# Exact 16-bit row reordering, wide sums over slots and a new step order in a four-layer graph kernel

## The chip, the cores and the metric

The kernel runs on one core of a Trainium2 chip. The metric is the device time of one execution in microseconds, the median over runs. PE is the matrix engine (TensorE; PEld is its loading of weights), DVE the vector engine, ACT the scalar engine, POOL the GpSimd engine, and SP the engine that here only issues transfers.

## The reference

Sixteen graphs (batches) of N = 1024 nodes with C = 64 channels go through four graph layers. Each layer is added to its input and followed by a layer norm over the 64 channels. The adjacency `adj` is 16 x 1024 x 1024, not symmetric in its values, symmetric in its pattern, with the diagonal set and below one per cent of the other entries filled.

```python
x = layernorm(x + (adj @ (x @ W0) + b0))                       # layer 0
# layer 1: Chebyshev, K = 4
z0, z1 = x, adj @ x;  z2 = 2*adj @ z1 - z0;  z3 = 2*adj @ z2 - z1
x = layernorm(x + sum(z_k @ theta[k]))
# layer 2: for each node the multiset of its neighbours' rows (diagonal included);
# where there are over 10 neighbours, every skip-th edge is dropped, in both directions
agg = 0.25*quantile(rows, 0.25) + 0.5*quantile(rows, 0.5) + 0.25*quantile(rows, 0.75)
x = layernorm(x + mask * (relu((x + agg) @ W1 + b1) @ W2 + b2))
# layer 3: batch norm over all 16 * 1024 rows, then (I - D^.5 adj D^-.5)
x = layernorm(x + leaky_relu((I - An) @ (batchnorm(x) @ W3 + b)))
```

The quantiles are taken in each channel by itself, with linear interpolation between sorted values, so layer 2 has to fetch the rows of each node's neighbours and sort them.

## The kernel before

Nodes are tiled as 8 chunks (`NK`) of 128 partitions. One batch passes through nine generators, each of which issues its instructions in steps that end in a `yield`:

- `rows in` loads the adjacency by rows of chunks, turns it on PE (L476) and evacuates it on ACT (L477) into `f_adj_t`, kept in fp32. For each chunk ACT also makes a key of the row's signs (L497), DVE multiplies it by a band of node numbers (L499) and takes the largest eight of each 128 columns (L502), which gives each node's list of neighbours.
- `layers` computes layers 0 and 1. A product with the adjacency is a "hop" (L451): 16 fp32 matmuls of 512 moving columns, `f_adj_t` moving and the node values as weights. Its last step norms the rows into `xr` and writes them to DRAM as `rows`.
- `lists` turns each node's neighbours into a record of row numbers, sorts the nodes by their number of neighbours, and computes each node's `place`. Steps `at0` to `at7` make a one-hot matrix on DVE for each chunk (L701, f16, 128 x 1152), with which PE moves the records (L705) and the node rows `xr` (L725) into the sorted order. For L725 ACT first casts the one-hot to fp32 (L722). Step `ids` (13) copies the row numbers out (L736 is the copy of `meta`); step `own` (14) turns the reordered rows into `xs`.
- `fetch` issues the gathers on POOL (L768): indirect transfers of 128 rows each from `rows`, 70 in a batch (3 + 12 in steps 0 to 2, 37 in steps 3 to 10, 18 in steps 11 to 14).
- `heads` prepares the gathered rows: dead slots, interpolation weights, and the copies on ACT (L839) from the gather buffers `got` into `home`. A next batch's gather into the same buffer waits for these.
- `sorts` sorts the slots on DVE, 128 partitions at a time (L869), in three classes of chunks (1, 4 and 3 chunks, with 24, 11 and 8 slots), multiplies by the weights (L883), and sums over the slots on PE (L893) into the PSUM bank `xt`. There the slots' values are the weights of the array (64 or 128 columns, one or two chunks), and a scaled identity of 128 columns moves: the sum comes out already turned, with channels on partitions.
- `ends` copies `xt` (L908), runs the perceptron of layer 2 (L913 and on) and norms into `x3p`.
- `back` undoes the sorting: a row of places, eight one-hots on DVE (L961, f16), a cast on ACT (L963), and two fp32 matmuls (L966) for each. The last step copies the result, channels on partitions, into `f_x3t` (L971).
- `third` loads the turned adjacency again from DRAM (step 0), scales the rows into the weights `u` (step 1, L994 and on, with the statistics L988), does the hop of layer 3 (step 2, copied by ACT at L999), scales (step 3) and writes out (step 4).

All instructions are issued in one written order. Step u of generator g in batch b has the due time `b * PERIOD + WHEN[g][u]`, and the steps of all batches are issued sorted by it:

```python
for name, part in (...):
    parts += [(b * PERIOD + when, b, name, u, part) for u, when in enumerate(WHEN[name])]
for _, b, name, u, part in sorted(parts, key=lambda p: p[0]):
    next(part)
```

The due times only set the order of each engine's queue; nothing waits for a clock. `PERIOD` is 120 in units of the plan. A step that is written earlier on an engine holds all that follow on it until its inputs are there. Around the release of the gathers of batch b the order is: `lists[b]` 13, `back[b-2]` 7 to 10, `lists[b+1]` 1 and 2, `sorts[b-1]` 83 to 110 with `lists[b]` 14, `third[b-2]` 1, `layers[b+1]` 1 and 2, `lists[b+1]` 3, `heads[b-1]` 7 among them, then `third[b-2]` 2 (the hop) and `rows in[b+2]` 1.

Each PSUM bank name stands for one bank, except for two banks each of `l0` and `turn`; `end` serves `ends`, `back` and `third`. The buffers `at16` and `at32` have two copies each.

After the last batch the batch norm and the final norm of all batches follow ("fin", L1619 to L1712), with POOL doing two 128 x 512 operations a batch (L1689, L1705). A slow path for graphs with too many neighbours is built in and not taken with these inputs.

Of the kernel before, what the change touches and what calls it, by code (L numbers as in the profile page):

```python
# [10 lines left out]
F32 = mybir.dt.float32  # L11
# [8 lines left out]
P = 128  # L20
# [155 lines left out]
def _strides(slots):  # L176

    out, rest = [], list(slots)
    while rest:
# [13 lines left out]
PERIOD = 120  # L193

WHEN = {
    "rows in": (-248.4, -220, -217.5, -211.2, -206.1, -201.4, -197.3, -189.6, -181.9, -172.4),
    "layers": (-135.2, -116.7, -104.1, -98.7, -95, -86.9, -83, -79.2, -69.6, -67.9, -63, -56.1),
    "lists": (-134.5, -130.9, -129, -114.6, -64.7, -48, -48, -39.8, -39.8, -34.9, -31.5, -24.3, -19.3, -14.4, -4.6),
    "fetch": (6.9, 14.8, 29.3, 29.3, 29.3, 33.6, 39.4, 42.9, 72, 72, 88.8, 96.5, 105.4, 108, 110.5),
    "heads": (41.2, 50.2, 51.6, 89.4, 102.9, 106.2, 109.8, 132.9, 144.8, 154.8),  # L200
    "sorts": (
        58.3, 58.3, 58.3, 59.6, 59.6, 63.2, 64.7, 64.7, 64.7, 64.7, 64.7, 64.7, 64.7, 64.7, 64.7, 64.7, 72.1, 74.9,
        75.8, 76.2, 76.2, 76.2, 76.2, 76.2, 76.6, 76.6, 76.6, 76.6, 78.4, 78.7, 78.7, 79.6, 79.9, 80.5, 80.8, 80.8,
        80.8, 84.4, 85, 85, 85.9, 86.4, 86.4, 87.6, 87.6, 87.6, 88.5, 89.1, 89.1, 89.1, 89.1, 89.8, 89.9, 89.9,
        90.9, 90.9, 90.9, 91.6, 91.6, 91.6, 91.6, 91.6, 92.6, 92.7, 95.1, 95.1, 95.1, 95.2, 95.2, 98.6, 98.6, 98.6,
        99.6, 100.6, 101.1, 102.8, 103, 103, 103, 103, 103, 103, 103, 112.3, 113, 113.3, 113.3, 120.9, 122.3, 127,
        127, 129.6, 129.6, 133.4, 134.1, 134.1, 134.1, 135.8, 137.3, 137.3, 137.3, 137.3, 137.3, 137.3, 137.3,
        137.3, 137.3, 137.3, 137.3, 137.3, 137.3, 141.1, 141.1, 141.1, 141.1, 141.1, 146.8, 157.7, 157.7, 158, 158,
        158, 158, 158, 159.1, 162.4, 163.6, 163.6, 163.6, 165.1, 168.3, 168.3, 169.2, 172.4,
    ),  # L210
    "ends": (181.3, 188.1, 197.1, 207.7),
    "back": (149.8, 155.7, 209.3, 209.7, 211.2, 212.4, 212.9, 228, 229.8, 231.4, 231.4),
    "third": (222.8, 241.8, 258.3, 262.5, 291.8),
# [4 lines left out]
def gnn_layers_kernel(  # L218
# [261 lines left out]

# [43 lines left out]
    def layers(b, st, pw):  # L524
# [60 lines left out]
        nc.scalar.dma_start(out=rows[N : N + 1], in_=big_row)  # L585
        st.update(rows=rows)
        yield "rows"

    def lists(b, st, pw):

        mask = mask_t[:, b * NK : (b + 1) * NK]
# [1151 lines left out]
```

## Time and profile before

| what | value |
|---|---|
| median of 14 runs | 2976.2 us (2961.8 to 2981.37) |
| profiled execution, its own time | 2961.18 us |
| its span in the profile | 2959.4 us |
| mean granted clock of PE | 0.772 |
| busy: PE, DVE, ACT, POOL | 1880.9, 1889.4, 1457.0, 1195.3 us |
| gathers (L768 into `got`) | 1072, 1034 ns each |
| casts to fp32 (L722, L963) | 128 + 128, 1042 ns each |

The profile is of one execution. Busy times are summed over all instructions of an engine, without the instructions that only wait, branch or issue transfers. A row of the groups of instructions gives line, engine, operation, what is written from what, shape and count, then the busy time in us and the mean of one in ns, then the engine's idle time just before these instructions with what ended it. "Issue" as a releaser is time in which the engine waited for nothing that the profile shows, "remote" an event that could not be put to an instruction. An fp32 matmul of this kernel is recorded as two records, so the 512 records of L725 are 256 matmuls. The windows by stage give, for a stretch of the span, the busy time and the number of instructions of each engine, the granted clock, the share of busy DMA engines and their GB/s.

### The profile page before, as it was taken

The page shows a single profiled execution, that of the slowest core. Times are in us where ns is not written, and L with a number is a line of the kernel's source. Part 1 is how long each engine was busy: PE and PEld are TensorE (multiplying, and loading weights), DVE is VectorE, ACT ScalarE, POOL GpSimd, SP SyncE. Part 2 cuts the span into 40 slices and gives each one's busy share as a digit, 9 for nine tenths or more (in the row PEclk, how much of TensorE's full clock was granted, in tenths as well). Part 3 has the DMA queues.
Part 4 walks back from the last instruction along what each step waited for, and adds up shares of the span by engine and source line. Part 5 has one row for each costly group of instructions (what it writes and reads, how often), then busy time and mean ns, then how long its engine had stood idle before and what let it go on. Part 6 is the DMA issues. An engine that isn't in the chain of part 4 may idle for free. (4 is left out here: it accounts for less than half of the span.)

```text
span 2959.4 us, 33419 instructions
## 1 busy us (share of the span) xinstructions
PE 1880.9 (64%) x9766; PEld 950.6 (32%) x9766; DVE 1889.4 (64%) x5870; ACT 1457.0 (49%) x4405; POOL 1195.3 (40%) x1159
## 2 busy tenths in 40 slices
PE   5727366776758485775848576675848677663553
PEld 3303242423324152332414242342415243232233
DVE  6507576684939487584938567593948668372826
ACT  4505355563736365463726456373726556362533
POOL 0260725436162725426162633616162543626004
PEclk9957687887969697786958788786969788776675
DMA  4322232242424133242414124242414223121126
GB/s 160 119 40 104 43 126 68 60 151 53 154 46 164 31 117 95 60 150 49 156 43 165 35 73 137 59 148 47 162 31 144 69 61 133 21 77 30 58 81 160
DMA packets 130464, 272.28 MB, mean 92 GB/s; under 512 B 77024, under 2 KB 77280, under 8 KB 120032
## 3 DMA queue, kind: packets, MB, share of 16 engines
q1 hardware_dynamic: 57536, 218.90, 19.9%
q0 software_dynamic: 35840, 37.92, 8.2%
q10 hardware_dynamic: 36896, 13.23, 1.8%
q8 instruction: 79, 1.29, 0.2%
q14 instruction: 113, 0.93, 0.1%
HBM read 185.89 MB, written 84.07 MB: 91 GB/s over the span
## 5 line engine op out<-in xcount | busy, mean ns | idle before, releaser
L768 POOL DMA_INDIRECT got<-rows,ids x1072 | 1108.5, 1034 | 559.0 <-issue 252.2
L451 PE MATMUL ps_end<-f_adj_t,f_u 128*64 128x512 f32 x512 | 263.1, 853 | 332.8 <-issue 297.6
L768 POOL DMA_INDIRECT extra<-rows,more x48 | 49.0, 1021 | 1019.4 <-ACT meta L736 1009.7
L499 DVE TENSOR_TENSOR key<-key,keyband 128x1024 f16<-128x1024 f16 x128 | 88.4, 690 | 534.2 <-ACT key L497 524.7
L451 PE MATMUL ps_l<-f_adj_t,f_t 128*64 128x512 f32 x1536 | 371.6, 631 | 34.5 <-issue 34.5
L839 ACT ACTIVATE home<-got,big 128x64 f32<-128x64 f32 x1344 | 332.5, 338 | 0.0
L476 PE MATMUL ps_turn<-cf,f_a 128*128 128x128 f32 x1024 | 190.8, 323 | 185.9 <-issue 158.9
L869 DVE TENSOR_TENSOR away<-home 128x768 f32<-128x768 f32 (+9 forms) x416 | 230.6, 574 | 46.1 <-ACT home L839 21.8
L476 PEld LDWEIGHTS ps_turn<-cf,f_a 128*128 128x128 f32 x1024 | 138.0, 163 | 271.8 <-issue 230.8
L451 PEld LDWEIGHTS ps_end<-f_adj_t,f_u 128*64 128x64 f32 x512 | 59.0, 181 | 510.9 <-issue 472.0
L477 ACT COPY f_adj_t<-ps_turn 128x512 f32<-128x512 f32 x256 | 139.3, 595 | 169.1 <-PE ps_turn L476 74.9
L502 DVE MAX8 cand<-key 128x8 f16<-128x128 f16 x1024 | 210.8, 280 | 5.3 <-issue 0.9
L966 PE MATMUL ps_end<-at,f_h 128*64 128x512 f32 x512 | 149.3, 684 | 91.2 <-issue 48.9
L999 ACT COPY f_ht<-ps_end 128x512 f32<-128x512 f32 x16 | 9.4, 586 | 393.8 <-remote 238.3
L725 PE MATMUL ps_px<-at,xr 128*64 128x512 f32 x512 | 176.7, 776 | 31.8 <-ACT at L722 31.3
L451 PEld LDWEIGHTS ps_l<-f_adj_t,f_t 128*64 128x64 f32 x1536 | 113.4, 145 | 258.8 <-issue 256.5
L893 PE MATMUL ps_xt<-quarter,home 128*128 128x128 f32 (+1 forms) x1088 | 165.5, 290 | 17.8 <-DVE home L883 17.8
L869 DVE TENSOR_TENSOR home<-away,home 128x128 f32<-128x128 f32 (+5 forms) x352 | 165.5, 474 | 9.5 <-remote 2.7
L893 PEld LDWEIGHTS ps_xt<-quarter,home 128*128 128x128 f32 (+1 forms) x1088 | 140.7, 185 | 44.2 <-DVE home L883 41.6
L722 ACT CAST at<-at 128x1024 f32<-128x1024 f16 x128 | 130.4, 1042 | 49.5 <-DVE at L701 31.9
L497 ACT ACTIVATE key<-f_a 128x1024 f16<-128x1024 f32 x128 | 136.2, 1064 | 33.5 <-DVE cand L502 18.1
L869 DVE TENSOR_TENSOR home<-away 128x64 f32<-128x64 f32 (+7 forms) x304 | 149.2, 509 | 1.1
(236 smaller groups left out, 3335.6 us busy)
## 6 DMA issues: line engine op xcount, KB each, us to landing
f_a<-in_adj_dram SPq DMA_DIRECT2D x128, 512.0 KB
adj<-f_adj_t SPq DMA_DIRECT2D x16, 4096.0 KB
f_adj_t<-adj SPq DMA_DIRECT2D x64, 1024.0 KB
got<-rows,ids POOLq DMA_INDIRECT x1072
rows<-xr ACTq DMA_DIRECT2D x16, 264.0 KB
f_x<-in_x_dram ACTq DMA_DIRECT2D x16, 256.0 KB
x_d<-f_x SPq DMA_DIRECT2D x16, 256.0 KB
z_d<-f_ht SPq DMA_DIRECT2D x16, 256.0 KB
```

Source lines behind the costliest of these rows:

```text
L451: nc.tensor.matmul(ps[h * C : (h + 1) * C, :], lhsT=v[:, j, :], rhs=pairs[:, j, h], start=(j == 0), stop=(j == NK - 1),)
L476: nc.tensor.transpose(pt[:, j * P : (j + 1) * P], a[:, (4 * g + j) * P : (4 * g + j + 1) * P], ident)
L477: nc.scalar.copy(adj_t[:, 4 * g : 4 * g + 4, i * P : (i + 1) * P], pt.rearrange("p (j n) -> p j n", n=P))
L497: nc.scalar.activation(flat_key, a, AF.Sign)
L502: nc.vector.max(out=cand[:, i, j * 8 : j * 8 + 8], in_=key[:, j, :])
L722: nc.scalar.copy(at_32, at_place[:, 0:N])
L725: nc.tensor.matmul(po[h * C : (h + 1) * C, :], lhsT=xr[:, k, 0:C], rhs=pairs[:, h], start=(k == 0), stop=(k == NK - 1))
L768: nc.gpsimd.indirect_dma_start(out=w[0], out_offset=None, in_=rows[:, :], in_offset=bass.IndirectOffsetOnAxis(ap=w[1], axis=0))
L839: nc.scalar.activation(home[:, s + 1, k, :], got[:, s, k, 0:C], AF.Identity, bias=big_dead[:, s, k : k + 1], scale=1.0,)
L869: nc.vector.tensor_tensor(out=at(ho, r1 if is_max else r0, *run), in0=at(ha, r0, *run), in1=at(hb, r1, *run), op=ALU.max if is_max else AL ...
L893: nc.tensor.matmul(st["xt"][h * C : (h + n) * C, q * P : (q + 1) * P], lhsT=flat(xs[:, k : k + n, :] if s == nr else home[homes[s]][:, s, ...
L966: nc.tensor.matmul(ps[h * C : (h + 1) * C, :], lhsT=x3p[:, k, :], rhs=pairs[:, h], start=(k == 0), stop=(k == NK - 1))
```

## The change

Three things are changed.

First, the reordering in `lists` and `back` no longer casts the one-hot to fp32. The rows are split instead into three bf16 terms whose sum is the fp32 value exactly: the upper 16 bits of each number, read in place; the upper 16 bits of the rest (`mid`); and what is left (`low`). POOL computes the two differences (`in_three`), in a new last step of `layers` for `xr` and in the last step of `ends` for `x3p`. `reordered` then issues for each chunk six matmuls with a bf16 term as weights and the f16 one-hot moving.

Second, the sums over slots in `sorts` keep the scaled identity as weights and move all chunks of a class at once (64, 256 or 192 columns). The sum now comes out with nodes on partitions, so `ends` gets a new first step `summed`, which copies the bank and turns it on PE before the perceptron; the order of chunks in the perceptron's matmuls follows.

Third, `PERIOD` becomes 110 and all due times are new; `layers` and `ends` have one step more. Around the release of the gathers of batch b the order is then: `lists[b]` 13 and 14, `back[b-2]` 10, `layers[b+1]` 1, `lists[b+1]` 2, `sorts[b-1]` 84 to 112 with `third[b-2]` 1, `fetch[b]`'s first steps, `back[b-1]` 0, `lists[b+1]` 3 and `layers[b+1]` 2 among them, then `third[b-2]` 2 and `rows in[b+2]` 1. The two POOL steps lie at 57.5 (`layers` 12) and 63.7 (`ends` 4) of the period of 110, with `fetch` 10 and 11 between them.

```diff
-PERIOD = 120
+PERIOD = 110
 
 WHEN = {
-    "rows in": (-248.4, -220, -217.5, -211.2, -206.1, -201.4, -197.3, -189.6, -181.9, -172.4),
-    "layers": (-135.2, -116.7, -104.1, -98.7, -95, -86.9, -83, -79.2, -69.6, -67.9, -63, -56.1),
-    "lists": (-134.5, -130.9, -129, -114.6, -64.7, -48, -48, -39.8, -39.8, -34.9, -31.5, -24.3, -19.3, -14.4, -4.6),
-    "fetch": (6.9, 14.8, 29.3, 29.3, 29.3, 33.6, 39.4, 42.9, 72, 72, 88.8, 96.5, 105.4, 108, 110.5),
-    "heads": (41.2, 50.2, 51.6, 89.4, 102.9, 106.2, 109.8, 132.9, 144.8, 154.8),
+    "rows in": (-220.5, -212.9, -206.9, -203.9, -199.1, -190.5, -182, -178.6, -172.8, -161),
+    "layers": (-122.6, -117.9, -111.4, -102.8, -96.5, -91.4, -84.2, -73.4, -69.9, -66, -64.6, -60.7, -52.5),
+    "lists": (-127.9, -124, -117.5, -113, -95.9, -50.7, -49.5, -43.5, -39.9, -39.9, -39.5, -35, -19.2, -10.1, -10.1),
+    "fetch": (-4.2, -2.9, -2.9, 7.2, 9, 34.9, 51.2, 51.2, 51.2, 54.6, 62.1, 63.1, 68.7, 68.7, 94.1),
+    "heads": (18.9, 37.8, 38.3, 70.2, 76, 76.2, 84.2, 117.4, 134, 135.7),
     "sorts": (
...
     ),
-    "ends": (181.3, 188.1, 197.1, 207.7),
-    "back": (149.8, 155.7, 209.3, 209.7, 211.2, 212.4, 212.9, 228, 229.8, 231.4, 231.4),
-    "third": (222.8, 241.8, 258.3, 262.5, 291.8),
+    "ends": (155.2, 157.2, 158.6, 168, 173.7),
+    "back": (106.3, 175.1, 185.4, 193.9, 197.8, 199.3, 201.3, 201.7, 208.5, 208.5, 210.4),
+    "third": (207, 215.2, 224.8, 232.6, 245.1),
 }
@@ -478,6 +478,30 @@
 
     flat = lambda t: t.rearrange("p k c -> p (k c)")
 
+    def upper(t, n=C):
+        return t.bitcast(BF16)[:, :, 1 : 2 * n : 2]
+
+    def in_three(pw, x, tag):
+
+        mid = pw.tile([P, NK, C], F32, name=f"{tag}_mid")
+        nc.gpsimd.tensor_tensor(out=mid, in0=x[:, :, 0:C], in1=upper(x), op=ALU.subtract)
+        low = pw.tile([P, NK, C], BF16, name=f"{tag}_low")
+        nc.gpsimd.tensor_tensor(out=low, in0=mid, in1=upper(mid), op=ALU.subtract)
+        return upper(x), upper(mid), low
+
+    def reordered(ps, parts, hot, k):
+
+        pairs = hot.rearrange("p (q h n) -> p h q n", h=2, n=P)
+        for i, part in enumerate(parts):
+            for h in range(2):
+                nc.tensor.matmul(
+                    ps[h * C : (h + 1) * C, :],
+                    lhsT=part[:, k, :],
+                    rhs=pairs[:, h],
+                    start=(k == 0 and i == 0),
+                    stop=(k == NK - 1 and i == 2),
+                )
+
     def rows_in(b, st, keyband, pa, pw):
 
         x0 = pw.tile([P, NK, C], F32, name="f_x0")
@@ -585,6 +609,8 @@
         nc.scalar.dma_start(out=rows[N : N + 1], in_=big_row)
         st.update(rows=rows)
         yield "rows"
+        st.update(x_parts=in_three(pw, xr, "x"))
+        yield "parts"
 
     def lists(b, st, pw):
 
@@ -718,13 +744,7 @@
                 stop=(k == NK - 1),
             )
 
-            at_32 = pw.tile([P, N], F32, name="at32", bufs=2)
-            nc.scalar.copy(at_32, at_place[:, 0:N])
-            pairs = at_32.rearrange("p (q h n) -> p h q n", h=2, n=P)
-            for h in range(2):
-                nc.tensor.matmul(
-                    po[h * C : (h + 1) * C, :], lhsT=xr[:, k, 0:C], rhs=pairs[:, h], start=(k == 0), stop=(k == NK - 1)
-                )
+            reordered(po, st["x_parts"], at_place[:, 0:N], k)
             yield f"at{k}"
         ids = pw.tile([P, NK, OTHERS], I32, name="ids", bufs=AHEAD + 2)
         nc.scalar.copy(ids, pr[:, :, 0:OTHERS])
@@ -884,28 +904,25 @@
 
             if "xt" not in st:
                 st["xt"] = bank("xt")
-            k = k0
-            while k < k0 + nk:
-                n = 2 if k % 2 and k + 1 < NK else 1
-                q, h = ((k - 1) // 2, 0) if n == 2 else (NK // 2 - 1, 1 if k else 0)
-                cols = slice(k - k0, k - k0 + n)
-                for s in range(nr + 1):
-                    nc.tensor.matmul(
-                        st["xt"][h * C : (h + n) * C, q * P : (q + 1) * P],
-                        lhsT=flat(xs[:, k : k + n, :] if s == nr else home[homes[s]][:, s, cols, :]),
-                        rhs=ident if s == nr else quarter,
-                        start=(s == 0),
-                        stop=(s == nr),
-                    )
-                k += n
+            for i in range(nr + 1):
+                nc.tensor.matmul(
+                    st["xt"][:, k0 * C : (k0 + nk) * C],
+                    lhsT=ident if i == nr else quarter,
+                    rhs=flat(xs[:, kk, :] if i == nr else home[homes[i]][:, i]),
+                    start=(i == 0),
+                    stop=(i == nr),
+                )
             yield f"sums{k0}"
 
     def ends(b, st, pw):
 
         meta, xs = st["meta"], st["xs"]
         xt = st.pop("xt")
+        xn = pw.tile([P, 512], F32, name="f_ht", bufs=2)
+        nc.scalar.copy(xn, xt)
+        yield "summed"
         xt_s = pw.tile([P, 512], F32, name="f_h")
-        nc.scalar.copy(xt_s, xt)
+        nc.scalar.copy(xt_s, turned(xn, "xt"))
         ht = []
         for h in range(2):
             hp = slice(h * C, (h + 1) * C)
@@ -923,7 +940,7 @@
             stop=False,
         )
         for k in range(NK):
-            h, q = {0: (0, 3), 7: (1, 3)}.get(k, (1 - k % 2, (k - 1) // 2))
+            h, q = k % 2, k // 2
             nc.tensor.matmul(
                 ph[:, k * C : (k + 1) * C], lhsT=ht[h][:, q * P : (q + 1) * P], rhs=w2_c[:, 0, :], start=False, stop=(k == NK - 1)
             )
@@ -934,7 +951,7 @@
         nc.vector.tensor_tensor(out=h, in0=h, in1=xs, op=ALU.add)
         x3p = h
         yield from norm(pw, x3p, [h], "n2", centred=True)
-        st.update(x3p=x3p)
+        st.update(x3p=in_three(pw, x3p, "x3"))
         yield "x3p"
 
     def back(b, st, pw):
@@ -959,13 +976,7 @@
         for k in range(NK):
             at_node = pw.tile([P, N + P], F16, name="at16", bufs=2)[:, 0:N]
             nc.vector.tensor_scalar(out=at_node, in0=row, scalar1=node[:, k : k + 1], scalar2=None, op0=ALU.is_equal)
-            at_32 = pw.tile([P, N], F32, name="at32", bufs=2)
-            nc.scalar.copy(at_32, at_node)
-            pairs = at_32.rearrange("p (q h n) -> p h q n", h=2, n=P)
-            for h in range(2):
-                nc.tensor.matmul(
-                    ps[h * C : (h + 1) * C, :], lhsT=x3p[:, k, :], rhs=pairs[:, h], start=(k == 0), stop=(k == NK - 1)
-                )
+            reordered(ps, x3p, at_node, k)
             yield f"order{k}"
         xt = pw.tile([P, 512], F32, name="f_x3t")
         nc.scalar.copy(xt, ps)
```

## The prediction

> **What bounds the kernel now.** I read the busy times first, then the waits, then the windows by stage, and last the groups of instructions with their forms.
>
> The busy times of the whole span name no bound: no engine is above 64%.
>
> ```profile
> PE 1880.9 (64%) x9766; PEld 950.6 (32%) x9766; DVE 1889.4 (64%) x5870; ACT 1457.0 (49%) x4405; POOL 1195.3 (40%) x1159
> ```
>
> So the kernel must have stages with different bounds. The step `ids` (L736) of a batch releases the gathers of that batch (L768); call its time T. In the trace it ends at 128.3 for the first batch and at 2636.5 for the last: a period of (2636.5 - 128.3) / 15 = 167.2 us. The windows cut one period (T = 1471 to the next T = 1639) and the end of the one before it.
>
> ```profile
> engine line waited for: us in total, times, longest us
> POOL extra L768 <- ACT meta L736: 1009.7, 16, 122.9
> DVE key L499 <- ACT key L497: 524.7, 35, 56.5
> PEld ps_end L451 <- issue: 472.0, 310, 5.9
> ...
> PE ps_end L451 <- issue: 297.6, 159, 5.5
> POOL got L768 <- ACT home L839: 248.6, 54, 15.0
> ACT f_ht L999 <- remote: 238.3, 9, 48.5
> ```
>
> ```profile
> 1376.00:1471.00 95.00, 81.54 (x501) 43.28 (x501) 85.23 (x287) 68.73 (x201) 20.89 (x18) 0.92 0.41 146
> 1471.00:1495.00 24.00, 12.44 (x68) 7.36 (x66) 19.59 (x54) 14.32 (x46) 18.62 (x18) 0.70 0.24 47
> 1495.00:1545.00 50.00, 21.33 (x41) 5.66 (x42) 9.38 (x19) 6.22 (x27) 33.29 (x35) 0.57 0.15 24
> 1545.00:1639.00 94.00, 79.57 (x474) 41.09 (x474) 80.77 (x267) 63.76 (x179) 21.15 (x18) 0.89 0.41 147
> ```
>
> The columns are PE, PEld, DVE, ACT and POOL busy, the granted clock, the DMA share and GB/s. Three parts are seen. From T to T+24 all engines work. From T+24 to T+74 POOL runs gather after gather while PE ends 41 matmuls in 50 us and ACT 27 instructions; PE waits for nothing that the profile shows ("issue"), in the hop of `third` at L451. In the trace single records of that hop lie 2.8 us apart, and the copy behind it (ACT L999) is released at T+73.7 in every steady batch. Behind L999 in ACT's queue stands the key activation L497, and DVE stands at L499: 524.7 us over 16 batches. From T+74 to the next T (94 us) the work is dense: DVE is busy for 81 to 85 of 94, PE for 80, ACT for 64 to 69. DVE bounds this part, at 0.88 of its time.
>
> What ends the stall? The unbroken stream of gathers has 52 in a steady batch, 61 in the second and 70 in the first; L999 is released at T+73.7, T+86.6 and T+98.6: about 1.41 us for each gather, plus 0.4. The streams of 9 gathers later in the period, with breaks between, slow the others by 2 to 4 us only. I infer that a long stream of gathers slows the issue of the other engines; the trace shows the coincidence and not the mechanism.
>
> So period = stall end + (DVE's work of a batch - what DVE did before the stall end) / 0.88. In the period shown DVE did 19.59 + 9.38 = 29.0 before the stall end: 74 + 80.77 / 0.86 = 168.
>
> **Part by part.**
>
> ```profile
> L768 POOL DMA_INDIRECT got<-rows,ids x1072 | 1108.5, 1034 | 559.0 <-issue 252.2 <-ACT home L839 248.6 <-DMA got<-rows,ids 46.0
> L725 PE MATMUL ps_px<-at,xr 128*64 128x512 f32 x512 | 176.7, 776 | 31.8 <-ACT at L722 31.3
> L963 ACT CAST at<-at 128x1024 f32<-128x1024 f16 x128 | 130.5, 1042 | 21.1 <-DVE at L961 8.5 <-issue 4.9 <-PE ps_end L966 3.7
> L722 ACT CAST at<-at 128x1024 f32<-128x1024 f16 x128 | 130.4, 1042 | 49.5 <-DVE at L701 31.9 <-PE ps_px L725 17.2
> L893 PE MATMUL ps_xt<-quarter,home 128*128 128x128 f32 x704 | 102.2, 294 | 1.9 <-DVE home L883 1.8
> L908 ACT COPY f_h<-ps_xt 128x512 f32<-128x512 f32 x16 | 9.6, 600 | 17.6 <-remote 9.4 <-PE ps_xt L893 8.2
> L1689 POOL TENSOR_TENSOR hf<-hf,s 128x512 f32<-128x512 f32 x16 | 16.7, 1042 | 178.2 <-ACT s L1685 178.2
> ```
>
> The casts go: 16 in a batch at 1042 ns, 16.7 us of ACT. They lie in the dense part, where ACT has 25 to 30 us idle, so their direct worth is nothing; DVE's own waits for them are small (10.3 us in all at L961, 4.5 at L701, 0.9 a batch). If DVE were not the cover, they would be worth the full 16.7.
>
> The reordering matmuls: four f32 records for each k become six of one pass each. In bursts the trace places 32 f32 records of 512 columns in 7.1 us, 0.22 each, and the four of L725 take 1.1 us. For one-pass matmuls of 512 columns no burst is shown; the ends are 0.11 (half of the f32 pace) and 0.22, so six take 0.65 to 1.3. I take 0.65: two passes make one f32 product. PE gains 0.45 x 16 = 7 us a batch, or loses 3.5. It has 14 us free in the dense part, so either end costs at most 1 us.
>
> The sums: 112 records a batch become 76, wider by up to 4 times in columns. The old bursts place 40 records of 128 columns in about 5 us; the new ones move in total nearly the same columns. I take -2 us of PE, hidden as well (ends -5 and +3).
>
> `ends`: a copy like L908 (0.60) and four transposes (a batch of four f32 transposes is about 0.9 us apart from start to end, single records up to 0.42), with their hand-overs, lengthen the chain by 2.5 us. DVE has the sorts of the next batch queued beside it; I take 0, and 2.5 if that cover is gone.
>
> `in_three`: four POOL instructions of 128x512 a batch at 1042 ns (L1689), 4.2 us, perhaps 6 with the strided 16-bit operand. POOL is idle for 70 of the 94 us of the dense part. At0's matmuls (`lists` 5) wait on two of them, and order0's on the other two; what is queued behind those matmuls on PE is delayed by 2 to 3 us once each if POOL is just then in a gather. I take 1 us a batch, ends 0 and 6.
>
> Against these instructions speaks a rule of the Trainium skill ("SBUF — State Buffer", section on the two separate sides): VectorE and GpSimd share one pair of ports as an exclusive lock, taken for a whole instruction when a VectorE operation has two SBUF inputs and the GpSimd operation reads SBUF. The trace shows something like it on POOL's side only: gathers start 1.25 us apart while DVE idles and up to 1.8 while it works, and DVE's own 128x768 steps take 953 or 967 ns without and with gathers. By the rule, DVE would be held for all of POOL's 4.2 us in a batch, 63 us over 15 periods.
>
> The new order matters most, since it decides what stands in front of the stall. DVE's queue between `ids` and the first L499 block held, before: three one-hots of L961 (1.4), `lists` 1 and 2 (5.5), `sorts` 83 to 110 (19.9), the norm's and the heads' small steps (3.0): 29 to 30. After: only `lists` 2 (3.0), `sorts` 84 to 112 (19.2), the small steps (2.5 to 3): 25. The stream after `ids` is 50 gathers instead of 52 (`lists` 13 and the fetch steps stand so that two steps of gathers come later), so the stall ends at 1.41 x 50 + 0.4 = T+71, 2.8 us sooner. And PE has less in front of the hop: `back` 7 to 9 with its matmuls and casts is done before `ids`. The hop can start at about T+14 instead of T+21 to T+25, and takes 7 to 10 us at full pace. The slow part began at T+24 in steady batches. If the hop is through by then, L999 no longer holds ACT's queue; `rows in` 1, `heads` 7 and `sorts` 113 to 114 run too, some 7 us of DVE, and 32 are done by T+71.
>
> The sum, likeliest case: stall end -2.8, dense part -(32 - 29) / 0.88 = -3.4, POOL +1: -5.2 a period, 15 periods -78. At the ends of the run I count +5: the last batch's unbroken stream is 5 gathers longer (+6.7) and `ends` +2.5, `back` -4. The profiled execution took 2961.2 (span 2959.4): 2961 - 73 = 2888. The median of the runs shown is 2976.2, 1.005 of it, so 2888 x 1.005 = 2903; I say 2905. With 1 us either way in each of the three terms it reaches from 2865 to 2945.
>
> **The rivals.**
>
> *The hop is still caught (slower).* Its weights u come from ACT steps after `third` 1, which in the trace lag by 1 to 5 us at T+12 to T+20. If it has not ended when the slow part begins, L999 holds ACT until T+71, and only 25.5 us of DVE work lie in the stall: -2.8 + 3.5 / 0.88 + 1 = +2.2 a period, +33, +5 at the ends: 2999, times 1.005 = 3014; with 1 us either way 2990 to 3035. It decides from a hop end later than T+24. For it speaks that batch 0's slow part began at T+8 to T+18, with DVE idle; against it that steady batches have DVE busy then.
>
> *POOL's instructions hold others.* Streams of 7 and 13 gathers, with `in_three` between and without the pauses for L839, could slow the dense part as the last unbroken 18 gathers did in this trace (a gap of 10 us on DVE). At 5 to 10 us a period: 3050 to 3130. Against it speak the short gaps beside 9 gathers.
>
> *The dense part shrinks with the plan.* If ACT's and PE's relief lets DVE run at 0.95 of the dense part instead of 0.88, that part loses a further 6 us a period: 2800 to 2830. Against it: DVE's waits there are 4 us of small pauses and few waits for ACT.
>
> *It does nothing:* terms cancel, 2970 to 2982.
>
> **How the numbers follow.** The likeliest case, 0.45; the plan's case, 0.10; the hop caught, 0.30; POOL in the way, 0.10; nothing, 0.05. Faster by over 0.2%: the first two, and a sliver of the third, 0.56. Within 0.2% (6 us, about what a measurement of this kernel can tell from no change): 0.06. Slower: 0.38. The range leaves out the plan's case for the most part and POOL's: 2830 to 3035.
>
> **What would show it.** Right: the period between two `ids` is 161 to 163; L999 is released before T+25; L497 is no longer held until the gathers end; the first L499 runs inside the stream; DVE's busy time between T and T+71 is 31 to 33. The 256 casts are gone and ACT's busy time falls by about 250 us without the span following. The reordering takes 0.65 us for each k. Wrong: L999 still lies at T+71 with 25 us of DVE before it (the first rival), DVE gaps beside POOL's TENSOR_TENSOR or DVE steps that last 1 us longer (the second), or a stall end that does not follow the number of gathers: then the term of 1.41 us each fails and all cases move.

## The result and the profile after

The changed kernel takes 3237.6 us, the median of 10 runs (3228.8 to 3267.8), against 2972.8 for the kernel before over 47 runs: 1.090 times the time before, with a 95% interval of 1.088 to 1.093. It was forecast at 2905, between 2830 and 3035. The profiled execution took 3274.1 (span 3272.3). Here and below, runs that took over 1.5 per cent longer than the fastest run of the same kernel are left out of times and ratios.

The busy times of the profile after:

```profile
PE 1847.8 (56%) x9766; PEld 1015.2 (31%) x9766; DVE 1946.9 (59%) x5870; ACT 1207.2 (37%) x4165; POOL 1249.5 (38%) x1223
```

ACT has lost its 256 casts and 250 us, DVE has gained 58 us, and the span has grown by 313. In this section and below, T is the end of ACT's copy of `meta` (L756 after, L736 before), which releases a batch's gathers. The period between two T is 194.5 in the steady part (167.2 before). The windows of one period from T = 1421 (the last 7 us left out), columns as in the prediction:

```profile
1421.00:1445.00 24.00, 11.55 (x83) 8.37 (x83) 16.31 (x50) 4.10 (x17) 18.48 (x18) 0.83 0.16 24
1445.00:1497.00 52.00, 23.17 (x71) 9.36 (x72) 14.71 (x29) 8.72 (x30) 32.12 (x33) 0.58 0.24 52
1497.00:1541.00 44.00, 28.43 (x146) 15.94 (x144) 41.40 (x138) 29.73 (x92) 0.00 (x0) 0.87 0.23 78
1541.00:1555.00 14.00, 13.91 (x62) 8.75 (x63) 0.31 (x2) 1.45 (x3) 0.00 (x0) 0.81 0.00 0
1555.00:1594.00 39.00, 25.75 (x189) 14.21 (x190) 37.25 (x115) 20.57 (x83) 15.86 (x15) 0.83 0.64 232
1594.00:1609.00 15.00, 2.80 (x23) 1.15 (x21) 1.49 (x6) 7.99 (x34) 8.88 (x10) 0.61 0.14 23
```

The stall of before is still there and ends within a microsecond of where it did, at T+76 (DVE's key step L523 starts at T+75.8, L499 before at T+75.3): 31.0 us of DVE work lie ahead of its end, against 29. What is new are two holes in what was the dense part. From 1541 to 1555 PE is busy without a break and DVE does 0.31 us. From 1594 to 1609 DVE does 1.49 us and PE 2.80. The timelines of PE and DVE around the first hole show a chain (start, duration, engine, line, operation, and in brackets the idle time before with what ended it):

```profile
1529.35 1.11 PE L476 MATMUL ps_turn<-cf,f_a 128*128 128x128 f32 x8
1541.09 1.01 PE L908 MATMUL ps_xt<-away,quarter 128*128 128x192 f32 x2 [10.63 <-DVE away L903]
...
1546.42 7.09 PE L451 MATMUL ps_l<-f_adj_t,f_t 128*64 128x512 f32 x32
```

```profile
1540.49 0.82 DVE L903 TENSOR_TENSOR away<-away,wts 128x384 f32<-128x384 f32 x2
1555.13 0.69 DVE L523 TENSOR_TENSOR key<-key,keyband 128x1024 f16<-128x1024 f16 x1 [13.82 <-ACT key L521]
```

In the new order step 8 of `layers` (its third hop) stands behind `sorts` 131 to 133, the last of which is the sum over slots of the third class. PE waits 10.6 us for DVE's weighting (L903), does the sum (5.4) and then the hop (7.1). ACT's copy of the hop and, behind it, the key activation L521 follow. DVE has nothing queued ahead of that key: it idles for 13.8 us while PE works, after PE had idled for 10.6 while DVE worked.

The second hole, in DVE's timeline:

```profile
1598.03 0.52 DVE L727 TENSOR_SCALAR at<-columns,place 128x1152 f16<-128x1152 f16 x1 [3.96 <-remote]
1608.10 0.49 DVE L978 TENSOR_SCALAR at<-row,node 128x1024 f16<-128x1024 f16 x1 [9.55 <-remote]
```

By the program, DVE's next one-hot waits for a buffer of `at16` (two, shared by `lists` and `back`), whose last reader is now a PE matmul; before, it was ACT's cast or the few matmuls of the records. PE had ended its matmuls on the two buffers at 1593.2 and 1594.6. Its signals for them (updates of a semaphore, the counter by which one engine tells another that it is done; the trace records them too) come at 1598.0 and 1608.0, and DVE starts within 0.1 us of each. So DVE waits for late signals of PE, not for PE's work. POOL's last 13 gathers ran without a break from 1589.4 to 1605.6, and DVE goes on 2.5 us after their end. These 13 and 7 more came late, since POOL's queue had stood for 85 us at the first subtraction, waiting for `xr`, with the last 20 gathers of the batch behind it.

Two groups of DVE's waits carry this over the whole span (us in total, times, longest):

```profile
DVE key L523 <- ACT key L521: 493.8, 49, 39.8
...
DVE at L978 <- remote: 152.1, 19, 11.0
```

Summed over the seven steady periods from the sixth batch on, with overlapping instructions counted once, DVE's period before was 114.2 us busy, 8.2 of gaps under 0.8 us and 46.3 of longer ones (168.6). After, it is 117.8, 6.5 and 69.7 (194.0). So of the 25 us a period 23.4 are longer waits and 3.6 are longer instructions.

Most of the 3.6 has a cause of its own, seen where POOL's subtractions run (POOL's timeline, then DVE's):

```profile
1572.19 1.50 POOL L487 TENSOR_TENSOR x_mid<-xr 128x512 f32<-128x512 f32 x1 [85.32 <-ACT xr L437]
1573.77 1.30 POOL L489 TENSOR_TENSOR x_low<-x_mid 128x512 bf16<-128x512 f32 x1
```

```profile
1574.10 1.05 DVE L889 TENSOR_TENSOR home<-away 128x64 f32<-128x64 f32 x1
1575.19 0.29 DVE L889 TENSOR_TENSOR away<-away 128x64 f32<-128x64 f32 x1
```

A sorting step of 128x64 that takes about 0.22 us takes 1.05 while `x_low` is computed, and ends with it. Over all DVE instructions that overlap a subtraction the excess over the median of the same form is 2.9 us a batch.

### The profile page after: what moved, and what is told of

It reads as the page before. It is cut to its first block, busy times and chain, and to the rows that moved or that the text cites. A ratio compares the mean times of both kernels' runs of the same rounds, so it can differ in the third digit from the quotient of the medians.

```text
span 3272.3 us, 32447 instructions
## 1 busy us (share of the span) xinstructions
PE 1847.8 (56%) x9766; PEld 1015.2 (31%) x9766; DVE 1946.9 (59%) x5870; ACT 1207.2 (37%) x4165; POOL 1249.5 (38%) x1223
## 5 line engine op out<-in xcount | busy, mean ns | idle before, releaser
L788 POOL DMA_INDIRECT got<-rows,ids x1072 | 1086.9, 1014 | 335.1 <-issue 309.9
L487 POOL TENSOR_TENSOR x_mid<-xr 128x512 f32<-128x512 f32 x16 | 23.3, 1456 | 1289.0 <-ACT xr L437 1176.8
L451 PE MATMUL ps_end<-f_adj_t,f_u 128*64 128x512 f32 x512 | 243.6, 852 | 302.8 <-issue 298.1
L523 DVE TENSOR_TENSOR key<-key,keyband 128x1024 f16<-128x1024 f16 x128 | 87.9, 687 | 520.5 <-ACT key L521 493.8
L908 PE MATMUL ps_xt<-home,quarter 128*128 128x256 f32 (+2 forms) x672 | 184.6, 420 | 62.2 <-DVE home L903 59.4
L476 PE MATMUL ps_turn<-cf,f_a 128*128 128x128 f32 x1024 | 159.3, 302 | 77.1 <-ACT f_adj_t L477 36.6
L908 PE MATMUL ps_xt<-away,quarter 128*128 128x64 f32 (+1 forms) x448 | 95.7, 342 | 159.1 <-DVE away L903 157.9
L908 PEld LDWEIGHTS ps_xt<-home,quarter 128*128 128x128 f32 x672 | 148.6, 249 | 97.9 <-DVE home L903 72.2
L731 PE MATMUL ps_l<-rec,at 128*128 128x26 f16 x1024 | 49.2, 182 | 213.3 <-DVE at L727 155.9
L978 DVE TENSOR_SCALAR at<-row,node 128x1024 f16<-128x1024 f16 x128 | 62.6, 499 | 170.2 <-remote 152.1
L497 PE MATMUL ps_end<-at,f_h 128*64 128x512 f16 x256 | 67.8, 509 | 163.0 <-DVE at L978 152.5
L1010 ACT COPY f_ht<-ps_end 128x512 f32<-128x512 f32 x16 | 9.4, 587 | 393.4 <-PE ps_end L451 287.7
```

The lines of the kernel that those rows point to most:

```text
L451: nc.tensor.matmul(ps[h * C : (h + 1) * C, :], lhsT=v[:, j, :], rhs=pairs[:, j, h], start=(j == 0), stop=(j == NK - 1),)
L476: nc.tensor.transpose(pt[:, j * P : (j + 1) * P], a[:, (4 * g + j) * P : (4 * g + j + 1) * P], ident)
L497: nc.tensor.matmul(ps[h * C : (h + 1) * C, :], lhsT=part[:, k, :], rhs=pairs[:, h], start=(k == 0 and i == 0), stop=(k == NK - 1 and i == 2),)
L523: nc.vector.tensor_tensor(out=flat_key, in0=flat_key, in1=keyband[:, off : off + N], op=ALU.mult)
L731: nc.tensor.matmul(pr[:, c, :], lhsT=at_place[:, c * P : (c + 1) * P], rhs=rec[:, k, :], start=(k == 0 and c == 0), stop=False,)
L788: nc.gpsimd.indirect_dma_start(out=w[0], out_offset=None, in_=rows[:, :], in_offset=bass.IndirectOffsetOnAxis(ap=w[1], axis=0))
```

## The experiments

Theory A: the new order makes the loss (the hop behind the sums, the late gathers). Theory B: the arithmetic makes it (POOL's subtractions, one-hots freed by PE). Later a third question came up: whether the stall beside the gathers has a part in it at all.

**Order and arithmetic apart.** The new arithmetic in the old order:

```diff
-PERIOD = 110            # and all due times of after
+PERIOD = 120            # and those of before, with
+    "layers": (..., -63, -56.1, -56.05),
+    "ends": (181.2, 181.3, 188.1, 197.1, 207.7),
```

> The new arithmetic (three 16-bit terms, POOL's four subtractions a batch, wide sums, the turn in ends) in the old order: PERIOD and all due times of before, the two new steps put directly beside their neighbours (layers 12 after layers 11, summed directly ahead of ends 1). Theory A, the new order is the loss: the period goes back to 164 to 168 us and the time lies at 2920 to 2990, since 16.7 us less of ACT and some PE lie beside DVE. Theory B, the arithmetic is the loss (POOL's subtractions, one-hot buffers held by six matmuls, slower sums): most of the 265 us stays, 3150 or more.

It took 3064 (3047 and 3082) beside 2985.4, a ratio of 1.027 (1.015 to 1.038). Between the two theories: the order is not all. In its trace (of an execution of 3094) POOL's stream after `ids` is 40 gathers instead of 52; 10 and 20 come late, behind the subtractions, and the 20 end 2 to 4 us ahead of the next 40. DVE waits up to 50.5 us at L978.

The old arithmetic in the new order:

```diff
-PERIOD = 120            # and all due times of before
+PERIOD = 110            # and those of after; in layers and ends:
+        yield "parts"
+        yield "summed"
```

> The old arithmetic (ACT casts, fp32 matmuls, narrow sums) in the new order: PERIOD 110 and all new due times; the steps parts and summed do nothing. Theory A (order): about as slow as the changed kernel or slower, since the casts come back on ACT, 3200 to 3350, with DVE idle again for about 14 us at T+120 before L499. Theory B (arithmetic): 2950 to 3000.

3311.7, a ratio of 1.110 (1.100 to 1.119), inside the forecast of theory A. So the order alone costs 326 us, the arithmetic alone 79, and both together 265, each against the kernel before beside it: in the new order, the new arithmetic gains some 60. The split into three terms and the wide sums were not run apart, so what each has of the arithmetic's part is not shown. The trace has the hole before L499 (14.5 us at T+109) and 14 us at the one-hots, there with ACT's cast as the releaser. It also settles a step of the prediction. The hop of `third` got through in time here, its copy ran at T+22 to T+26 in every steady batch, and yet:

```profile
POOL extra L769 <- ACT meta L737: 1408.2, 16, 121.8
DVE key L499 <- ACT key L497: 650.8, 56, 63.6
PEld ps_l L451 <- issue: 583.5, 970, 8.4
```

L499 was held until T+75.5 all the same. PE was caught in the next hop, that of `layers` (ps_l), and in the transposes behind it, one record every 2 us. In the period from T = 1475 that hop's last record ends at T+43, and ACT's copy of it, with the next key behind it, starts at T+74.

**Each hole by itself.** The hop ahead of the sums:

```diff
-    "layers": (..., -84.2, -73.4, -69.9, -66, ...),
+    "layers": (..., -84.2, -73.4, -72.2, -66, ...),
```

> The changed kernel with one due time changed: the third hop of layers (step 8) at -72.2 instead of -69.9, so that PE does it ahead of the last sums over slots (sorts 133) and not behind them. In the changed kernel PE waits 10.6 us for DVE there, then does sums (5.4) and hop (7.0), and DVE is idle for 13.8 us until the copy of the hop and the key activation behind it are done. Theory A: those 13.8 us go in each of 14 periods, 3237 - 190 = 3045, at least 3100 if half of it is found again later. Theory B: under 30 us change.

3162.3, a ratio of 1.059 (1.048 to 1.070); the gain on the change is some 75 us (88 by the differences from the kernels before) and not 190. The one wait of 13.8 us is gone, but two waits for the same key stand at T+110 and T+131 (4.4 and 5.5). So 10 of the 13.8 us have only moved, and over the same seven periods the period is 4.8 us shorter (189.2). The second run, d2_hop_ahead_again, took 3212 on another chip (1.074, 1.067 to 1.081).

> e3_hop_ahead unaltered (the changed kernel with the third hop of layers ahead of the last sums). c1_change_again has one idle stretch of DVE a period left on the chip with 2191, 13.5 us before L523 behind sums and hop. If that is the order's whole price there, 2395 - 14 x 13.5 = 2205, 2190 to 2230. If the wait only moves, over 2300. On a chip with 2960 to 3000: 3140 to 3180.

It met a chip of the kind of the first runs, so its 2205 was not tested, and it lies above the 3140 to 3180 forecast for that kind.

The late gathers split:

```diff
-    "fetch": (..., 54.6, 62.1, 63.1, 68.7, 68.7, 94.1),
+    "fetch": (..., 54.6, 54.7, 54.8, 62.1, 68.7, 94.1),
```

> The changed kernel with the due times of fetch 10, 11, 12 and 13 changed to 54.7, 54.8, 62.1 and 68.7: the late gathers run as 7 ahead of the first pair of POOL subtractions, 5 between the pairs and 8 behind the second, instead of 7 and 13. If the unbroken stream of 13 is what holds DVE's one-hots (L727, L978: 13.5 us a period at T+173 to T+187, with PE's last matmul long done), 8 to 11 us a period go: 3237 - 130 = 3105, 3080 to 3140. If the one-hot chain through two buffers is slow by itself, under 30 us change.

3183.2, a ratio of 1.066 (1.056 to 1.077): 54 us less than the change (67 by the differences from the kernels before), about half of the forecast. The wait at L978 ("remote") fell from 152.1 to 63.9 us in all, but the first stream grew from 50 to 52, and in some periods the stretch behind it held DVE at L999 for 35 us; the periods lie between 176 and 201.

Both at once, with all gathers ahead of the subtractions:

```diff
-    "layers": (..., -73.4, -69.9, ...),    "fetch": (..., 54.6, 62.1, 63.1, 68.7, 68.7, 94.1),
+    "layers": (..., -73.4, -72.2, ...),    "fetch": (..., 54.6, 54.7, 54.8, 54.9, 55.0, 55.1),
```

> The changed kernel with the third hop of layers ahead of the last sums (step 8 at -72.2) and with fetch 10 to 14 at 54.7 to 55.1, all ahead of POOL's first pair of subtractions, so that no gather stands behind a subtraction that waits. The 20 late gathers then run between T+75 and T+125, held up by L859, and not at T+152 to T+184 beside the one-hots. If the order of POOL's queue and the hop are the loss, both idle stretches of DVE (13.8 and 13.5 us) go for the most part: a period of 170 to 178, 2930 to 3050. If the late gathers do the same harm where they are now, 3100 or more.

3096.9 (1.038, 1.019 to 1.057), between the two forecasts (up to 3050, and 3100 or more). A period had 177 to 181 us, the wait at the one-hots was gone, and two waits of 5 us for the key were left. On a second chip it took 3230.4, over 100 above its forecast:

> e5_ahead_both unaltered (hop ahead, and all gathers ahead of POOL's subtractions). On the chip with 2191: the same as d2 within 30 us, if late gathers do no harm where no engine is slowed; over 2300 if the subtractions behind 70 gathers come too late for PE. On a chip with 2960 to 3000: 3080 to 3110.

1.079 (1.075 to 1.084): there DVE was held at L999 and L432 longer, and the two waits for the key were 5 to 9 us each. One kernel, 130 us apart on two chips: on chips of this kind the size of a mended wait is not settled to better than that. The kernel before, traced on that second chip, had the period and the stall of the profile before:

> The kernel before, unaltered, for its trace beside the others of this call. On a chip with 2191: a period of 119 to 120 with DVE busy for 114 of it and idle stretches of 0.8 us or more under 2 us in all, where c1_change_again had 14. On a chip with 2960 to 3000: as the profile before.

2988.8, a period of 170.1 with 114.2 us of DVE work.

The new arithmetic in the old order, with POOL's queue as before:

```diff
-    "layers": (..., -56.1, -56.05),    "fetch": (..., 72, 72, 88.8, 96.5, 105.4, 108, 110.5),
+    "layers": (..., -56.1, -48),       "fetch": (..., 72, 72, 72, 72, 72, 72, 72),
```

> The new arithmetic in the old order as in e1_old_order, but with fetch 10 to 14 at 72, and the subtractions of xr directly ahead of at0 (layers 12 at -48), so that POOL issues all of a batch's gathers ahead of its four subtractions. In e1_old_order the stream after ids was 40 gathers and 10 + 20 came late; here it should be 52 + 9 + 9 as before. If the place of the subtractions in POOL's queue made e1_old_order slower than before, this is at 2930 to 2990. If the arithmetic itself is slower (six matmuls that hold the one-hot buffers, or DVE held by POOL), 3040 or more.

3199.2 (1.072, 1.056 to 1.088): it went the other way, to the second forecast. The streams are 52 and 18 (the two of 9 run as one), and DVE's list of waits is headed by one that the old arithmetic did not have:

```profile
ACT f_x3t L982 <- PE ps_end L497: 773.5, 13, 68.5
DVE at L978 <- remote: 773.3, 14, 61.0
```

In a steady period DVE stands at L978 from T+12 to T+73, and in that window (T = 1403) PE, DVE and ACT do next to nothing:

```profile
1415.00:1476.00 61.00, 6.08 (x22) 2.92 (x21) 0.21 (x3) 0.00 (x0) 40.29 (x43) 0.53 0.16 24
```

The old order has the last one-hots of `back` behind `ids`, in the first microseconds of the stream. In the profile before DVE had made the last of them by T+7.4, and ACT's cast had freed its buffer by T+10, ahead of the slow part. Now PE's six matmuls free the buffer. They came later and ended at T+16; the trace records PE's signal for them at T+73, and DVE starts at once. What costs DVE the 61 us is a signal that comes 57 us late.

**What the stream does.** Two kernels made from the kernel before. In the first, POOL pauses after each step of gathers:

```diff
             if n == 5 or n and w is None:
+                for _ in range(2):
+                    nc.gpsimd.memset(gots["pause"], 0.0)    # 128x1024 f32
                 n = 0
                 yield "gathers"
```

> The kernel before with two POOL memsets of 128x1024 after each step of gathers (2 to 5 gathers), some 2 to 4 us a step, so that no stream of gathers is longer than 5. If a long unbroken stream slows the other engines, the stall from T+24 to T+74 is thinned out: DVE runs at 0.8 or more there and the period falls from 167 to 130 to 150, 2400 to 2750. If every gather costs the others its 1.3 us wherever it stands, or if the stall is only the wait for the gathered data, the time stays or grows by the pauses: 2970 to 3200.

2302.0 beside 2991.8, a ratio of 0.772 (0.760 to 0.783), more than the first forecast gave. No stream is longer than 5, each memset takes 0.98 us, and DVE's wait at L499 falls from 524.7 us to 40.0:

```profile
PE 1703.1 (74%) x9766; PEld 911.1 (40%) x9766; DVE 1955.6 (85%) x5870; ACT 1456.5 (63%) x4405; POOL 1714.8 (74%) x1639
...
L774 POOL MEMSET pause<- 128x1024 f32 x480 | 469.7, 978 | 13.9
```

POOL does 520 us more, all the gathers are done, and the kernel is 690 us shorter. The stall is not made by what a gather costs, nor by waiting for its rows, but by gathers that follow each other without a break, on this chip. The second leaves gathers out:

```diff
+            if k0 == 1:    # the 37 gathers of the second class
+                left_out |= {id(w[0]) for w in wanted[-37:]}
```

> The kernel before with the 37 gathers of the second class (four chunks) left out of each batch; their buffer keeps its zeros, and all later work is done as before. The stream after ids falls from 52 to 15. If the stream causes the stall, L999 is released at about T+24 and not T+74, and the period falls by 40 to 45 us to about 125: 2300 to 2400. If the stall is something else (a chain of PE, ACT and DVE that only lies beside the gathers), the period changes by under 10 us.

2240.7, a ratio of 0.751 (0.740 to 0.762), and a period of 124.9 (168.6 before): the forecast of 40 to 45 us a period for a stall that the stream makes holds, on the chip of m1_pauses, and the time lies 60 us below its range.

**The change without the stall.** The four combinations, each with the pauses of m1_pauses:

> The changed kernel with the same two POOL memsets after each step of gathers, to be held against m1_pauses (old arithmetic, old order, pauses: 2302). Theory: the change loses only through long streams (one-hot buffers freed by PE, whose signals come late, and hop and sums one after the other behind a late start). Without streams its period is DVE's work, 119 us, plus small waits, 122 to 130, and the time 2220 to 2320, not over m1_pauses by more than 1%. Rival: the new order's chain (sums, hop, key) and POOL's subtractions cost without streams too: 2400 to 2600.

> e1_old_order (new arithmetic, old order) with the pauses. Theory: the arithmetic's loss in the old order (3088 against 2985) came from the one-hot's buffers, which PE frees late in a stream; without streams it is within 2% of m1_pauses, 2260 to 2340. Rival: the new arithmetic is slower by itself by the same 100 us: 2400.

> e2_new_order (old arithmetic, new order) with the pauses. If the new order was laid out for casts that are gone, DVE waits for ACT's casts at the end of the period (14 us in e2_new_order) here too, and the hop behind the sums costs up to 14 us: a period of 130 to 145, 2350 to 2600. If the new order is harmless without streams: 2260 to 2340.

> e5_ahead_both with the pauses: the changed kernel, hop ahead of the last sums, all gathers ahead of the subtractions in POOL's queue. POOL then needs 70 gathers (91 us) and 32 memsets (31 us) a batch ahead of the subtractions, which wait for xr. Theory: 2180 to 2280, since neither the hop nor late gathers hold DVE. Rival: the subtractions come later than PE needs them and PE holds the one-hots: over n1_change_pauses.

These four met a chip on which the kernel before takes 2191.1, without any pause in its gathers. They are therefore held against m1_pauses, run again on a chip of that kind:

> m1_pauses unaltered: the kernel before with two POOL memsets after each step of gathers. On a chip with the kernel before at 2960 to 3000: 2290 to 2310 again, which makes n1, n3 and n4 comparable to it. On one with the kernel before at 2191: 2280 to 2320, since the pauses then only lengthen POOL's work (32 memsets of 0.98 us, 31 us a batch) and delay gathered rows.

2298.8 there (1.049 times the kernel before), 2302.0 on the first chip: for this kernel with pauses the kind of chip makes no difference. All that follows has pauses: old arithmetic and old order 2299; new arithmetic, old order 2426.6; old arithmetic, new order 2669.7; both 2476.1; both with hop and gathers ahead 2591.1, where the subtractions, behind 70 gathers and their pauses, come too late. For n1, n3 and n2 the rival held, and n4 lies above both its forecasts: the arithmetic costs 128 us by itself, the order 371, both together 177.

The traces say where. Over the seven periods from the sixth batch on, the kernel before with pauses (c3) has 125.5 us a period: 117.0 of DVE work, 7.4 of small gaps and 1.2 of longer ones. The change with pauses (n1) has 139.9: 120.2, 5.8 and 13.9, and the 13.9 are all the wait behind the sums and the hop. With the hop and the gathers ahead (n2) that wait is 4.3 and 5.7 us, so 10 of it stay here too, and DVE waits 11.4 us for PE at its one-hots. The two waits over the whole span, n1 and then n2:

```profile
DVE key L523 <- ACT key L521: 219.3, 36, 14.0
DVE at L727 <- PE ps_px L497: 244.5, 36, 43.7
```

The change and the old order with the new arithmetic, without pauses, on the chip of c3:

> The changed kernel, unaltered. On a chip on which the kernel before takes 2960 to 3000 it should take 3230 to 3270 as before. On a chip like that of n1_change_pauses, where the kernel before took 2191: if the change loses only through slow stretches beside gathers, it takes 2040 to 2200 here, a period of 110 to 119 and not over the kernel before; if the order and the arithmetic cost in themselves, as n1_change_pauses (2476) may say, 2300 to 2500.

> e1_old_order unaltered: new arithmetic, old order, no pauses. On a chip with the kernel before at 2960 to 3000: 3050 to 3110. On one with the kernel before at 2191: 2170 to 2230 if the arithmetic is neutral where no engine is slowed; about 2400 if it costs by itself (n3_old_order_pauses had 2427).

The changed kernel took 2395.5 against 2190.6, a ratio of 1.0925 (1.090 to 1.095); c2 took 2364.2 (1.079, 1.076 to 1.081). So the change loses the same 9% on a chip without the stall. There its streams are 63 gathers long and no engine is seen to be slowed; the windows of one period show where DVE idles:

```profile
1045.00:1120.00 75.00, 53.04 (x290) 31.21 (x289) 71.17 (x213) 42.39 (x134) 57.85 (x53) 0.85 0.37 91
1120.00:1135.00 15.00, 14.68 (x69) 9.56 (x70) 1.21 (x3) 2.25 (x4) 0.00 (x0) 0.82 0.02 2
1135.00:1182.00 47.00, 31.96 (x246) 17.09 (x245) 44.99 (x145) 28.49 (x120) 22.53 (x22) 0.85 0.56 197
```

The middle row is the hop behind the sums again: PE busy for 14.68 of 15 us, DVE for 1.21. It is the only longer wait of this period (137.0 us; the mean of the seven is 137.5, with 117.7 busy, 5.7 of small gaps and 14.2 of longer waits). DVE does not wait at the late gathers' one-hots here. In c2 the longer waits are 13.5 us a period: about 4 at L978 for PE, 7.5 at L811 for gathered rows that stood behind a subtraction, the rest at L432. No trace of the kernel before was taken on such a chip; from its span of 2189 less the part outside the steady periods in c3 (2297 - 15 x 125.5 = 414) or in m2 (2240 - 15 x 124.9 = 366), over 15, its period is estimated at 118 to 122.

## Why the prediction was wrong

**The sum over the dense part failed.** The prediction wrote the period as stall end plus the rest of DVE's work at 0.88 of the time, and let the new order change only what stands ahead of the stall. After the change DVE works for 87 of the 119 us behind T+76, 0.73 (the windows shown and 6.75 of the last 7 us). The hop behind the sums (13.8) and the one-hots behind late gathers (13.5) are as much as the period grew (194.5 - 167.2 = 27.3); the 3.6 us that DVE's instructions are longer are made up by 2 us less of small gaps and 2 to 4 us less of other waits. The place of both could have been read from the new table: `layers` 8 at 40.1, written behind `sorts` 133 at 40.1 and ahead of `rows in` 7 at 41.4, is a hop that waits for DVE and has DVE's next input behind it, and `fetch` 10 to 14 stand behind `layers` 12. That the 13.8 us would go with the hop's place does not follow: in e3, e5 and n2 10 of them stayed. (The period that the prediction cut was an uneven one: the next T was 1644, not 1639.)

**The stall end did not follow the number of gathers.** With 50 gathers the hop's copy (L1010) was released at T+74 and not T+71. The stream ended at T+65.6, and 9 records of the hop were left for the time after it (to T+74.2), which took 6.2 us, the first of them still 1.4 us apart. Two of the three points behind the 1.41 us a gather were misread: the first two batches have no hop of `third` yet, and what is released at T+98.6 and T+86.6 is L556, a copy of `layers`. And the profile before shows that the end of the hop was not what released L999. In its twelve steady batches with a hop the last record ends between T+55.6 and T+64.7, and the copy starts at T+73.7 or T+73.8 in all of them. In the period from T = 1471 PE's signal for the hop is recorded at 1544.78, 10.4 us after the hop's last record ended; that record and the copy:

```profile
1533.38 1.01 PE L451 MATMUL ps_end<-f_adj_t,f_u 128*64 128x512 f32 x1 [1.78 <-issue]
1544.80 0.59 ACT L999 COPY f_ht<-ps_end 128x512 f32<-128x512 f32 x1 [24.51 <-remote]
```

**The hop was caught, and getting it through is worth nothing.** In the period shown it starts at T+44, not T+14: ACT's `xs` (L767) lagged by 10.4 us as early as T+10. So the first rival's event came in, with 31.0 us of DVE work ahead of the stall's end and not 25.5. But e2_new_order had the hop through by T+26 and the same stall end. The likeliest case was priced on a release that the next PE step takes away.

**POOL's queue was underpriced.** The term for `in_three` was 1 us a period, ends 0 and 6. The POOL rival had the right streams (7 and 13 gathers in the dense part) and 0.10 of the chances; its 5 to 10 us were 13.5 on a chip with the stall; in c1 DVE has no such wait. What the prediction did not count is why the 20 gathers stand there: they queue behind a subtraction that waits 85 us. The rule of the Trainium skill ("SBUF — State Buffer", on the two separate sides), that the two engines lock each other out for an instruction, gave 4.2 us a batch, and 2.9 were measured: DVE steps do wait for the subtraction's end, and some of POOL's time meets no DVE instruction. In the old order, where under half of the subtractions meet a DVE instruction, it is 1.5 (c2). The rule was nearer than the trace's gathers, which hold only POOL.

**What a cast frees.** The casts were costed at nothing because ACT had room. That part is right (-250 us of ACT, no gain). But the cast also freed the one-hot's buffer, early and on ACT; now it is freed by a signal of PE, and in a stream that signal comes late. The new wait of DVE for PE is 61 us in a period of e1c_old_order_gathers_first and about 4 in c2, without a stall. The prediction named no such wait.

**Right.** Six matmuls of a chunk take 0.65 us at the full clock (0.22 for a pair of halves in c1) and 1.3 at the half clock, at which about half of them run (0.43 a pair, granted clock 0.61 in the window of the one-hots), both ends as bounded. ACT lost its 250 us without the span following, and a DVE step beside a subtraction lasted 0.8 us longer, as the second rival's sign had it.

## What to carry to other kernels

When an order is written anew, walk each engine's queue step by step: a step that waits for engine X with X's next input behind it costs both engines in turn, whatever the busy shares say; changing its place can leave most of the wait (10 of 13.8 us here). When a cast or a copy is taken away, ask what it freed, and who frees it now. An instruction that waits on the engine that issues gathers delays all gathers behind it. Putting it behind them is no sure cure: the gathers ahead gained in e5_ahead_both on one chip and lost with pauses (2591 against 2476); another engine was not tried. On a chip that shows the stall, short streams of gathers gained most.

## What the hardware showed that was not expected

Streams of indirect gathers on POOL slow the other engines on some chips and not on others. On three chips the kernel before took 2963 to 3007, about as in its 47 earlier runs (2955 to 2996); on two others the same kernel took 2191, and in c1_change_again, from there, streams of 63 gathers run beside PE, ACT and DVE without a gap like the stall's. Each chip was met only once, so a difference between chips and one between times cannot be told apart. Two memsets (2 us) after every five gathers bring both kinds to 2299 to 2302. On a slowed chip m1_pauses takes 23% less time than the kernel before, and 29% less than the changed kernel's median; on the others it takes 5% more than the kernel before and 4% less than the changed one. On a slowed chip it is not only that PE issues slowly: its signals come late. In the profile after, 76 of the 931 recorded semaphore updates of PE come over 5 us after the instruction that gives them has ended; in c1_change_again none of 952 comes even 1 us late (the last two of each execution left out). The traces differ in one thing more. Those from slowed chips lack 15 to 24 per cent of DVE's semaphore updates, those with pauses too, and those from the other chips under 1 per cent; a releaser "remote" in the former can be a record that is missing. What differs between the chips, and through what a stream reaches the other engines, no run here shows.
